# A block stack on one core: order of pieces of 16 and 32 passes, shifted copies issued from ScalarE's queue, feed-forward norms on ScalarE

## The chip, the core and the metric

The kernel runs on one core of a Trainium2 chip. The core's engines work side by side, each through its own instructions in order, and wait for each other through semaphores: TensorE (PE, with its weight loads PEld), VectorE (DVE), ScalarE (ACT), GpSimd (POOL) and SyncE (SP), which here issues most DMA transfers. The metric is the device time of one execution in microseconds; the time before is the median of three runs.

## The reference

Sixteen sequences of 256 tokens, 128 wide, in float32, pass through four residual blocks: softmax attention, a mixture of experts, retention, and a stack of six layers. The change touches the stack alone. One layer of it, cut:

```python
def attn_layer(x, Wqkv, qs, ksc, Wo):
    q, k, v = split(x @ Wqkv)                  # 16 heads of 64
    q = l2norm(q) * qs; k = l2norm(k) * ksc
    q = q * cos * scale + rotate_half(q) * sin * scale
    k = k * cos * inv + rotate_half(k) * sin * inv
    # windows of 32 queries see their own 32 keys and the 32 before
    attn = softmax(where(mask, -max, 8 * q @ k.T))
    return (attn @ v) @ Wo

def ffn_layer(x, g, bln, W1, b1, W2, b2):
    xn = (x - mean) / sqrt(var + 1e-5) * g + bln
    a, gate = split(xn @ W1 + b1)              # 2 x 341
    return a * gelu(gate) @ W2 + b2

for i in range(6):
    x = attn_layer(shift_tokens(x), ...) + x
    x = ffn_layer(shift_tokens(x), ...) + x
```

`shift_tokens` moves half of the channels by one token.

## The kernel before, in words

The first three blocks run until about 778 us. Then the stack begins. A unit (`Unit`) is the attention of one sequence in one layer: 6 layers x 16 sequences = 96 units. A `Forward` is the feed-forward part of two sequences. Their work is cut into named steps (methods), and the order of all steps is written out by hand as the words of `ORDER`: `pqk.1.0:4` means method `pqk` with arguments 1 and 0 for unit 2j + 4, in turn j of the loop (j from -3 to 50). One turn thus handles two sequences, each word at its own depth in the pipeline, and the engines' queues follow this order. The steps:

- TensorE: `pqk` (L916) makes queries or keys of four heads; `nr` (L950) sums the squares for the norms; `pv` (L994) makes values; `s_` (L1028) the scores, many small passes of 32 x 32; `pt` (L1083) transposes the probabilities; `o` (L1106) multiplies them with the values, in passes of 64 x 64; `y` (L1125) projects back. Of the feed-forward: `fn` (L1151) transposes, `trf` (L1185) transposes the normed values, `fg`, `fa` (L1204, L1217) and `fy` (L1234) are its three products. Each float32 matmul other than a transpose appears as two passes in the trace; `s_` and `o` as called before are 32 matmuls each, 64 passes, as is one `nr`.
- VectorE: `t2` and `rot` (L930, L935) for the rotation, `sm`, `mx`, `su`, `rec`, `nm` for the softmax, `rnA` and `rnC` for the norms, `xsu` (L1135) and `xsf` (L1249) add to the residual; `st` (L1163) takes the feed-forward's statistics and `z` (L1179) applies them.
- ScalarE: `sq` (L924) squares, `exp` (L1063), `rnB` (L965, a square root), `gl` (L1210, gelu), and copies out of PSUM: `vc` (L1003) values, `pTc` (L1091) probabilities, `oTc` (L1118) outputs, `nat` (L1157), `fz` (L1191).
- GpSimd: `add` (L941), `norm` (L988), `sub` (L1059), `rs` (L1169).
- SyncE's DMA queue: `bcD` (L975, L981) spreads a unit's norms over the partitions through DRAM, nine transfers; `vs` (L1010) copies parts of the values into a second place shifted by one window of 32 tokens, four transfers of 32 partitions per call, two calls a unit; and the weights of the next layer (`load_*`, issued by `follow` when the last user of the old ones has been emitted).

What couples them: `o` of the first half of a sequence's tokens reads what `vs.0` copied, of the second half also `vs.1`. PSUM is full: `pqk` has two buffers, scores one (so the scores of one half of the heads wait for `sm` of the other), `o` one, and everything else (`pt`, `pv`, `nr`, `y`, `fn`, `trf`, `fg`, `fa`, `fy`) takes turns in two buffers of `ps_m`: the third to come waits until the first has been read out. The readers of one `pqk` tile (`sq`, `t2`, `rot`) follow each other. Transfers signal on eight semaphores in rotation, and each issue waits until the transfer eight before it has landed.

Of the kernel before, what the change touches and what calls it, by code (L numbers as in the profile page):

```python
# [111 lines left out]
def kernel(ctx: ExitStack, tc: tile.TileContext, a: dict, widths: dict, out: bass.AP):  # L112
# [762 lines left out]
        nc.sync.dma_start(out=w, in_=a["wo2"][l].rearrange("p (c n) -> p c n", c=8))  # L875
        return w

    def load_ff(l):
        w1 = kc.tile([P, 2 * FF], F32, tag="w1", name=f"w1_{l}")
        w2 = kc.tile([P, 3, D], F32, tag="w2", name=f"w2_{l}")  # L880
        nc.sync.dma_start(out=w1, in_=a["w1"][l])
        nc.sync.dma_start(out=w2[:, 0:2, :], in_=a["w2"][l, 0:256].rearrange("(c p) n -> p c n", p=P))
        nc.sync.dma_start(out=w2[0 : FF - 256, 2, :], in_=a["w2"][l, 256:FF])
        return w1, w2

    class Unit:
# [55 lines left out]

        def nr(self, part):
            nr = self.misc("nr")[:, 0:64]
            for b in range(4 * part, 4 * part + 4):
                for hf in range(2):
                    for G in range(4):
                        nc.tensor.matmul(  # L950
                            nr[32 * G : 32 * G + 32, :],
                            lhsT=gather[:, b, :],
                            rhs=self.squares(G)[:, :, hf, WIN * b : WIN * b + WIN],
                            start=(b == 0 and hf == 0),
                            stop=(b == 7 and hf == 1),
                        )
# [48 lines left out]
        def vs(self, tt):  # L1005
            v = self.v_t
            for r in range(4):
                rows = slice(32 * r, 32 * r + 32)
                at, n = 2 * tt, 1 if tt and r % 2 else 2
                nc.sync.dma_start(out=v[rows, 1, at + r % 2 : at + r % 2 + n], in_=v[rows, 0, at : at + n])  # L1010

        def p_s(self, hu):
            return self.tile(ps_s, [P, 2, 2, 2, 2, 2 * WIN], "s", hu, tag="s")

        def s_(self, hu, tt, gh):
            ps, qk = self.p_s(hu), self.qk_t
            for G in (2 * gh, 2 * gh + 1):
                for hf in range(2):  # L1020
                    for b in range(4):
                        for r2 in range(2):
                            rows = slice(32 * (2 * hu + r2), 32 * (2 * hu + r2) + 32)
                            at = WIN * (4 * tt + b)
                            keys = qk[G][rows, 1, hf, at : at + 2 * WIN]
                            if b % 2 == 0:
                                keys = keys.rearrange("f (n t) -> f n t", n=2)[:, ::-1, :]
                            nc.tensor.matmul(  # L1028
                                ps[32 * b : 32 * b + 32, r2, tt, G // 2, G % 2, :],
                                lhsT=qk[G][rows, 0, hf, WIN + at : 2 * WIN + at],  # L1030
                                rhs=keys,
                                start=(hf == 0),
                                stop=(hf == 1),
                            )


        def t_sm(self, hu):
# [56 lines left out]
        def p_o(self, tt):  # L1094
            return self.tile(ps_o, [P, 2, 4, P], "o", tt, tag="o")

        def o(self, hu, tt):
            o, pT = self.p_o(tt), self.t_pT(hu, tt)
            for m in range(2):
                for b in range(4):  # L1100
                    for e in range(2):
                        for p in range(2):
                            rows = slice(64 * p, 64 * p + 64)
                            j = 2 * m + e
                            at = j * P + WIN * b
                            nc.tensor.matmul(  # L1106
                                o[64 * e : 64 * e + 64, p, 2 * hu + m, WIN * b : WIN * b + WIN],
                                lhsT=self.v_t[rows, 1 - b % 2, 2 * tt + b // 2, 4 * hu + j, :],
                                rhs=pT[rows, at : at + WIN],
                                start=True,  # L1110
                                stop=True,
                            )

        def t_oT(self):
            return self.tile(s2, [P, 8, T], "oT", bufs=1)
# [21 lines left out]
    class Forward(Unit):  # L1137
# [29 lines left out]
        def rs(self):  # L1167
            rs = self.tile(s2, [P, 4], "rs")
            nc.gpsimd.tensor_tensor(rs, rs, mhalf[:, 0:4], ALU.pow)  # L1169
            if self.last:  # L1170
                nc.sync.dma_start(out=self.tile(s2, [P, 4, D], "f_res", bufs=2), in_=kept[self.g])

# [1 line left out]
            return self.tile(s2, [P, 4, D], "ln_z")  # L1174

        def z(self):
            nat, mv, rs = self.t_nat(), self.tile(s2, [P, 4, 2], "ln_mv"), self.tile(s2, [P, 4], "rs")
            for k in range(4):
                nc.vector.tensor_scalar(  # L1179
                    self.t_z()[:, k, :], nat[:, k, :], mv[:, k, 0:1], rs[:, k : k + 1], ALU.subtract, ALU.mult  # L1180
                )

        def trf(self):
# [16 lines left out]

        def fg(self, n):
            f0, m = FFC[n]
            w1 = weights["ff", self.l][0]
            nc.tensor.matmul(  # L1204
                self.misc("fg", n)[0:m, :], lhsT=w1[:, FF + f0 : FF + f0 + m], rhs=self.t_zT(), start=True, stop=True
            )
# [6 lines left out]

        def fa(self, n):
            f0, m = FFC[n]
            w1 = weights["ff", self.l][0]
            nc.tensor.matmul(  # L1217
                self.misc("fa", n)[0:m, :], lhsT=w1[:, f0 : f0 + m], rhs=self.t_zT(), start=True, stop=True
            )
# [12 lines left out]
        def fy(self):  # L1232
            for n, (_, m) in enumerate(FFC):
                nc.tensor.matmul(  # L1234
                    self.misc("fy"),
                    lhsT=weights["ff", self.l][1][0:m, n, :],
                    rhs=self.t_h()[0:m, n, :],
                    start=(n == 0),
                    stop=(n == 2),
                )  # L1240
# [23 lines left out]


    ORDER = """
        add.1:3 o.0.0:0 sq.1.0:3 pqk.3.1:3 vs.1:0 fn:-2 rot.0.1:3 norm.1:2 pTc.1.1:0 t2.0.1:3 rot.3.1:3 sm.1:1
        sq.0.1:3 nat:-2 o.1.0:0 norm.0:2 rec.0:1 pqk.3.0:3 t2.3.0:3 oTc.0.1:0 pv.2:1 oTc.0.0:0 t2.3.1:3 o.0.1:0
        rot.3.0:3 pv.0:1 sq.3.1:3 s.0.0.0:2 add.0:3 sq.3.0:3 nm.0:1 mx.1:1 st:-2 vc.2:1 pqk.2.1:3 pv.3:1 sq.2.1:3
        o.1.1:0 pqk.2.0:3 vc.3:1 norm.3:2 sq.2.0:3 sub.1:1 norm.2:2 s.0.1.0:2 vc.0:1 t2.2.1:3 rot.2.1:3 pqk.1.0:4  # L1270
        pv.1:1 exp.1:1 nr.0:3 t2.2.0:3 nr.1:3 rs:-2 vc.1:1 su.1:1 rot.2.0:3 rec.1:1 rnA:3 rnB:3 pt.0.0:1 rnC:3 z:-2
        pqk.1.1:4 s.0.0.1:2 trf:-2 pTc.0.0:1 pt.0.1:1 s.0.1.1:2 fz:-2 pTc.0.1:1 nm.1:1 fy:-4 sm.0:2 oTc.1.0:0 bcD:3
        s.1.0.0:2 add.3:3 fg.0:-2 gl.0:-2 xsf:-4 t2.1.0:4 sq.1.1:4 s.1.1.0:2 t2.1.1:4 rot.1.0:4 mx.0:2 pt.1.1:1 pv.0:2
        pTc.1.1:1 vs.0:1 oTc.1.1:0 add.2:3 vc.0:2 s.1.0.1:2 rot.1.1:4 pt.1.0:1 y.0:0 sq.1.0:4 s.1.1.1:2 sub.0:2
        pqk.0.1:4 exp.0:2 norm.0:3 norm.1:3 pqk.0.0:4 sm.1:2 rot.0.1:4 o.0.0:1 sq.0.1:4 t2.0.1:4 add.1:4 su.0:2 y.1:0
        rec.0:2 xsu:0 pTc.1.0:1 mx.1:2 o.1.0:1 pv.3:2 t2.0.0:4 oTc.0.1:1 sub.1:2 pqk.3.1:4 nm.0:2 s.0.0.0:3 fa.0:-2
        oTc.0.0:1 rot.0.0:4 fh.0:-2 vc.3:2 sq.3.1:4 fg.1:-2 sq.0.0:4 exp.1:2 vs.1:1 o.0.1:1 fa.1:-2 o.1.1:1 rot.3.1:4
        pqk.3.0:4 gl.1:-2 t2.3.1:4 su.1:2 sq.3.0:4 norm.2:3 pqk.2.1:4 oTc.1.1:1 s.0.1.0:3 norm.3:3 rec.1:2 add.0:4
        fh.1:-2 pt.0.0:2 pTc.0.0:2 fg.2:-2 oTc.1.0:1 t2.3.0:4 s.0.1.1:3 pt.0.1:2 t2.2.1:4 rot.3.0:4 rot.2.1:4
        pqk.2.0:4 s.0.0.1:3 gl.2:-2 nm.1:2 pTc.0.1:2 sq.2.1:4 sq.2.0:4 sm.0:3 t2.2.0:4 rot.2.0:4 pv.1:2 vc.1:2 nr.0:4  # L1280
        mx.0:3 add.3:4 pqk.1.1:5 nr.1:4 rnA:4 pqk.0.0:5 s.1.1.0:3 t2.1.1:5 rnB:4 fa.2:-2 rnC:4 pv.2:2 bcD:4 sq.0.0:5
        sub.0:3 fh.2:-2 s.1.0.0:3 y.0:1 rot.1.1:5 sq.1.1:5 pqk.1.0:5 add.2:4 s.1.0.1:3 rot.0.0:5 t2.0.0:5 y.1:1
        exp.0:3 t2.1.0:5 vs.0:2 rot.1.0:5 vc.2:2 s.1.1.1:3 su.0:3 pt.1.0:2 pqk.0.1:5 xsu:1 pt.1.1:2 pTc.1.0:2
    """.split()

    weights = {}
# [10 lines left out]
    def follow(unit, method, args):  # L1297
# [11 lines left out]
        elif method == "t2" and q == 7 and count[key] == 1:  # L1309
            weights["rot", l + 1] = load_rot(l + 1)  # L1310
        elif method == "pv" and q == 9 and count[key] == 1:
            weights["v", l + 1] = load_v(l + 1)
        elif method == "y" and q == NSEQ - 1 and count[key] == 2:
            weights["o", l + 1] = load_o(l + 1)
        elif method == "fy" and q == NSEQ - 2:
            weights["ff", l + 1] = load_ff(l + 1)

    with tc.manual_schedule():
        for G in range(4):
# [1 line left out]
        weights["rot", 0] = load_rot(0)  # L1321
        weights["v", 0] = load_v(0)
        weights["o", 0] = load_o(0)
        weights["ff", 0] = load_ff(0)
        for j in range(-3, len(units) // 2 + 3):
            for method, args, d in steps:
                u = 2 * j + d
# [70 lines left out]
```

## Time and profile before

| | before |
|---|---|
| median of three runs | 4451.55 us (4458.10, 4432.63, 4451.55) |
| profiled execution, its own time | 4439.28 us |
| start of the first and of the last `pqk` | 778.1 and 4320.1 us |
| granted TensorE clock over the whole execution | 0.948 |
| ScalarE's table loads of `exp`, `rnB`, `gl` | 96, 95 and 93, 1.28 us each |
| DVE L1179 z, 192 of 128x128 | 90.0 us busy |
| DMA v<-v on SyncE's queue | 768 transfers, issue 507 ns at least, 582 in the middle |
| SyncE waiting for `rnC` (L968) ahead of `bcD` | 2084 us in all |

The share of an engine says how long it was busy, not that it set the end. In a list of waits a line reads: who waited, for whom, the microseconds in total, how often, and the longest. In a timeline each line has the start, the time, the engine, the line of code, the operation and the tiles, and in brackets the engine's idle time just before and what ended it; `x64` says that 64 instructions were merged. In a table of windows the columns are the stretch, its length, the busy time of PE, PEld, DVE, ACT and POOL (with counts), the granted TensorE clock as a share of full speed, the busy share of the DMA engines, and GB/s.

### The profile page before, as it was taken

The page shows a single profiled execution, that of the slowest core. Times are in us where ns is not written, and L with a number is a line of the kernel's source. Part 1 is how long each engine was busy: PE and PEld are TensorE (multiplying, and loading weights), DVE is VectorE, ACT ScalarE, POOL GpSimd, SP SyncE. Part 2 cuts the span into 40 slices and gives each one's busy share as a digit, 9 for nine tenths or more (in the row PEclk, how much of TensorE's full clock was granted, in tenths as well). Part 3 has the DMA queues.
Part 4 walks back from the last instruction along what each step waited for, and adds up shares of the span by engine and source line. Part 5 has one row for each costly group of instructions (what it writes and reads, how often), then busy time and mean ns, then how long its engine had stood idle before and what let it go on. Part 6 is the DMA issues. An engine that isn't in the chain of part 4 may idle for free.

```text
span 4437.5 us, 216472 instructions
## 1 busy us (share of the span) xinstructions
PE 4129.3 (93%) x100320; PEld 2826.1 (64%) x100320; DVE 2976.0 (67%) x5436; ACT 2078.2 (47%) x3342; POOL 2528.5 (57%) x1419
## 2 busy tenths in 40 slices
PE   5888886799999999999999999999999999999998
PEld 3555664466666666666666666666666666666665
DVE  4555553567777667776777676777677777667774
ACT  2334432244545445544455454455454555444543
POOL 2433333556666656665666666666666666666661
PEclk9879777789999999999999999999999999999999
DMA  3200000222222222222222222232322232222222
GB/s 114 79 27 22 14 6 9 69 67 58 63 63 62 66 69 62 58 67 62 64 66 61 69 55 56 65 74 49 75 51 74 55 75 58 64 59 65 65 65 51
DMA packets 208901, 260.85 MB, mean 59 GB/s; under 512 B 54143, under 2 KB 164605, under 8 KB 207101
## 3 DMA queue, kind: packets, MB, share of 16 engines
q1 hardware_dynamic: 204796, 243.38, 21.8%
q8 instruction: 787, 12.89, 1.3%
q10 hardware_dynamic: 3200, 3.62, 0.3%
q14 instruction: 118, 0.96, 0.1%
HBM read 140.98 MB, written 17.83 MB: 36 GB/s over the span
## 4 chain that ended last, share of the span: by engine, by line
PE 69%; DVE 10%; DMA 7%; POOL 5%; issue 3%; SPq 3%; ACT 3%; ACTq 0%; POOLq 0%; DVEq 0%
PE pqk L916 13%; PE s L1028 10%; PE o L1106 8%; PE pv L994 7%; PE y L1125 6%; DMA v<-v 4%; PE nr L950 4%; PE pt L1083 3%; PE fy L1234 3%; PE fa L1217 2%; PE fg L1204 2%; POOL qk L988 2%; PE st L271 2%; DVE sm L1077 2%; SPq L981 2%
## 5 line engine op out<-in xcount | busy, mean ns | idle before, releaser
L941 POOL TENSOR_TENSOR qk<-qk,t 128x1024 f32<-128x1024 f32 x384 | 907.1, 2366 | 303.7 <-DVE qk L935 299.6
L988 POOL TENSOR_TENSOR qk<-qk,bc 128x1024 f32<-128x1024 f32 x384 | 948.6, 2488 | 95.3 <-DMA v<-v 77.9
L1059 POOL TENSOR_TENSOR sm<-sm,mx 128x1024 f32<-128x1024 f32 x192 | 366.2, 1907 | 954.1 <-PE pt L1083 331.2
L916 PE MATMUL pqk<-xs,wqk 128*128 128x256 f32 x3072 | 847.7, 405 | 30.3 <-ACT sq L924 14.6
L1028 PEld LDWEIGHTS s<-qk 32*32 32x32 f32 x49152 | 537.1, 104 | 394.8 <-issue 371.4
L924 ACT ACTIVATE sq<-pqk 128x512 f32<-128x512 f32 x768 | 454.5, 599 | 688.0 <-DVE qk L935 364.9
L930 DVE TENSOR_TENSOR t<-pqk,rot 128x512 f32<-128x512 f32 x768 | 521.0, 685 | 279.3 <-ACT sq L924 135.5
L935 DVE TENSOR_TENSOR qk<-pqk,rot 128x512 f32<-128x512 f32 x768 | 514.6, 681 | 279.6 <-PE pqk L916 224.6
L1028 PE MATMUL s<-qk 32*32 32x64 f32 x49152 | 664.9, 223 | 16.8 <-POOL qk L988 7.5
L916 PEld LDWEIGHTS pqk<-xs,wqk 128*128 128x128 f32 x3072 | 546.4, 194 | 156.4 <-issue 56.0
L1106 PEld LDWEIGHTS o<-pT,v 64*64 64x64 f32 x24576 | 420.5, 139 | 289.6 <-issue 159.3
L1106 PE MATMUL o<-pT,v 64*64 64x32 f32 x24576 | 470.8, 224 | 77.3 <-DMA v<-v 76.0
L1091 ACT COPY pT<-pt 128x512 f32<-128x512 f32 x384 | 224.6, 585 | 446.2 <-PE pt L1083 235.9
L994 PE MATMUL pv<-wv,xs 128*64 128x512 f32 x1536 | 420.2, 626 | 0.0
L1077 DVE TENSOR_TENSOR sm<-sm,rec 128x1024 f32<-128x1024 f32 x192 | 418.7, 2181 | 0.0
L1125 PE MATMUL y<-oT,wo 128*128 128x256 f32 x1536 | 384.8, 394 | 0.3 <-ACT pT L1091 0.3
L1044 DVE TENSOR_TENSOR sm<-s,c_ident 128x1024 f32<-128x1024 f32 x192 | 233.9, 1218 | 143.0 <-PE s L1028 142.0
L1125 PEld LDWEIGHTS y<-oT,wo 128*128 128x128 f32 x1536 | 280.8, 193 | 43.9 <-ACT f_gl L1210 0.8
L1118 ACT COPY oT<-o 128x512 f32<-128x512 f32 x384 | 216.2, 589 | 160.7 <-PE o L1106 160.7
L1003 ACT COPY v<-pv 128x512 f32<-128x512 f32 x384 | 224.6, 585 | 131.2 <-PE pv L994 131.2
L286 POOL TENSOR_SCALAR_AFFINE_SELECT pe<-pe 128x512 f32<-128x512 f32 x128 | 81.7, 640 | 331.9 <-ACT pe L279 316.1
L1067 DVE TENSOR_REDUCE su<-sm 128x16 f32<-128x1024 f32 x192 | 232.4, 1210 | 38.7 <-ACT sm L1063 38.7
(188 smaller groups left out, 5298.5 us busy)
## 6 DMA issues: line engine op xcount, KB each, us to landing
bc<-ndr SPq DMA_DIRECT2D x768, 128.0 KB
v<-v SPq DMA_DIRECT2D x576, 128.0 KB
v<-v SPq DMA_DIRECT2D x192, 64.0 KB
rot_l<-in_rot_dram SPq DMA_DIRECT2D x12, 512.0 KB
rot<-rot_l SPq DMA_DIRECT2D x12, 512.0 KB
wqk<-in_wqk_dram SPq DMA_DIRECT2D x24, 256.0 KB
rot<-rot SPq DMA_DIRECT2D x6, 1024.0 KB
wv<-in_wv_dram SPq DMA_DIRECT2D x6, 512.0 KB
```

What stands on the lines that cost most here:

```text
L916: nc.tensor.matmul(self.p_qk(G, k)[:, hf, :], lhsT=weights["qk", G, self.l][:, k, hf, :], rhs=xq, start=True, stop=True)
L924: nc.scalar.activation(self.squares(G)[:, k], self.p_qk(G, k), AF.Square)
L930: nc.vector.tensor_tensor(self.t_2(G)[:, k], self.p_qk(G, k)[:, ::-1, :], weights["rot", self.l][:, 1, k], ALU.mult)
L935: nc.vector.tensor_tensor(self.qk_t[G][:, k, :, WIN : WIN + T], self.p_qk(G, k), weights["rot", self.l][:, 0, k], ALU.mult)
L941: nc.gpsimd.tensor_tensor(to, to, self.t_2(G), ALU.add)
L988: nc.gpsimd.tensor_tensor(to, to, self.bcast()[:, G, :, None, :].to_broadcast([P, 2, 2, T]), ALU.mult)
L994: nc.tensor.matmul(self.misc("pv", i)[64 * p : 64 * p + 64, :], lhsT=xs[self.g][:, self.s, cols], rhs=weights["v", self.l][:, p, :], start ...
L1028: nc.tensor.matmul(ps[32 * b : 32 * b + 32, r2, tt, G // 2, G % 2, :], lhsT=qk[G][rows, 0, hf, WIN + at : 2 * WIN + at], rhs=keys, start=( ...
L1059: nc.gpsimd.tensor_tensor(s3, s3, self.t_mx(hu)[:, :, None].to_broadcast([P, 16, 2 * WIN]), ALU.subtract)
L1077: nc.vector.tensor_tensor(s3, s3, self.t_rec(hu)[:, :, None].to_broadcast([P, 16, 2 * WIN]), ALU.mult)
L1106: nc.tensor.matmul(o[64 * e : 64 * e + 64, p, 2 * hu + m, WIN * b : WIN * b + WIN], lhsT=self.v_t[rows, 1 - b % 2, 2 * tt + b // 2, 4 * hu ...
L1125: nc.tensor.matmul(self.misc("y")[:, 0:T], lhsT=weights["o", self.l][:, ch, :], rhs=self.t_oT()[:, ch, :], start=(ch == 0), stop=(ch == 7),)
```

## The change

It does five things, all in the stack:

1. `s_`, `o` and `nr` are called for half as much each: `s_` for one group of heads (16 matmuls), `o` for one part (16), `nr` for two windows (16). Their matmuls are the same.
2. `vs` issues its four copies from ScalarE's queue.
3. `z` is four ScalarE activations with a scale and a bias in place of four VectorE operations; `rs` computes the bias with two more small GpSimd instructions.
4. `load_ff` is parted into `load_w1`, emitted after the layer's last `fg` or `fa`, and `load_w2`, emitted after `fy` as before.
5. `ORDER` is new: 243 words for 215. The depths still run from -4 to 5.

```diff
-            for b in range(4 * part, 4 * part + 4):
+            for b in (2 * part, 2 * part + 1):
...
-                nc.sync.dma_start(out=v[rows, 1, at + r % 2 : at + r % 2 + n], in_=v[rows, 0, at : at + n])
+                nc.scalar.dma_start(out=v[rows, 1, at + r % 2 : at + r % 2 + n], in_=v[rows, 0, at : at + n])
...
-        def s_(self, hu, tt, gh):
-            ps, qk = self.p_s(hu), self.qk_t
-            for G in (2 * gh, 2 * gh + 1):
-                for hf in range(2):
+        def s_(self, hu, tt, G):
+            ps, qk = self.p_s(hu), self.qk_t[G]
+            for hf in range(2):
...
-        def o(self, hu, tt):
+        def o(self, hu, tt, part):
             o, pT = self.p_o(tt), self.t_pT(hu, tt)
-            for m in range(2):
-                for b in range(4):
+            for b in range(4):
...
             nc.gpsimd.tensor_tensor(rs, rs, mhalf[:, 0:4], ALU.pow)
+            nb, mv = self.tile(s2, [P, 4], "nb"), self.tile(s2, [P, 4, 2], "ln_mv")
+            nc.gpsimd.tensor_tensor(nb, mv[:, :, 0], rs, ALU.mult)
+            nc.gpsimd.tensor_scalar(nb, nb, -1.0, None, ALU.mult)
...
             for k in range(4):
-                nc.vector.tensor_scalar(
-                    self.t_z()[:, k, :], nat[:, k, :], mv[:, k, 0:1], rs[:, k : k + 1], ALU.subtract, ALU.mult
+                nc.scalar.activation(
+                    self.t_z()[:, k, :], nat[:, k, :], AF.Identity, bias=nb[:, k : k + 1], scale=rs[:, k : k + 1]
                 )
...
-    def load_ff(l):
+    def load_w1(l):
...
+        elif method in ("fg", "fa") and q == NSEQ - 2:
+            both = (l, "w1")
+            count[both] = count.get(both, 0) + 1
+            if count[both] == 6:
+                weights["w1", l + 1] = load_w1(l + 1)
         elif method == "fy" and q == NSEQ - 2:
-            weights["ff", l + 1] = load_ff(l + 1)
+            weights["w2", l + 1] = load_w2(l + 1)
```

The new `ORDER`, its first and its last words (the seam between two turns) and the place of the even sequence's copies:

```
t2.3.1:3 rot.3.1:3 o.0.1.1:0 pqk.2.1:3 trf:-2 s.0.1.2:2 s.0.1.1:2 rot.2.1:3 sub.1:1 sq.2.1:3 vs.0:1 fz:-2
vs.1:1 pt.0.0:1 add.1:3 pqk.2.0:3 t2.2.1:3 s.0.0.1:2 s.0.1.0:2 add.3:3 pt.0.1:1 oTc.1.0:0 pqk.1.0:4 sq.2.0:3
pTc.0.0:1 nr.0:3 s.0.0.3:2 rot.2.0:3 pTc.0.1:1 sm.0:2 oTc.1.1:0 nr.1:3 mx.0:2 exp.1:1 y.0:0 nr.2:3 nr.3:3
...
oTc.1.1:1 mx.0:3 s.1.1.0:3 vs.0:2 s.1.0.1:3 y.1:1 sq.0.0:5 s.1.0.0:3 s.1.1.1:3 pqk.0.1:5 pt.1.0:2 s.1.0.2:3
xsu:1 s.1.1.3:3 pTc.1.0:2 rot.0.0:5 sub.0:3 vs.1:2 fa.2:-2 add.2:4 fn:0 t2.0.1:5 t2.0.0:5 o.0.0.1:2 rot.0.1:5
...
norm.2:4 s.0.0.2:4 rs:0 norm.3:4 pqk.3.1:5 nm.0:3 norm.0:4 pv.1:3 s.0.0.0:4 s.0.1.3:4 sq.3.1:5 pv.2:3
o.1.1.1:2 norm.1:4 vc.1:3 rot.3.0:5 vc.2:3 t2.3.0:5 z:0
```

and in the old one the even sequence's first copies and the first `o` that reads them, over the seam:

```
exp.0:3 t2.1.0:5 vs.0:2 rot.1.0:5 vc.2:2 s.1.1.1:3 su.0:3 pt.1.0:2 pqk.0.1:5 xsu:1 pt.1.1:2 pTc.1.0:2
add.1:3 o.0.0:0 ...
```

## The prediction

> **What bounds the kernel now.** I read the page first, then who waited for whom on TensorE in the steady part of the stack (1000 to 4250 us), then the timeline around the longest of those waits, then the granted clock in short stretches. The page:
>
> ```profile
> span 4437.5 us, 216472 instructions
> PE 4129.3 (93%) x100320; PEld 2826.1 (64%) x100320; DVE 2976.0 (67%) x5436; ACT 2078.2 (47%) x3342; POOL 2528.5 (57%) x1419
> PE 69%; DVE 10%; DMA 7%; POOL 5%; issue 3%; SPq 3%; ACT 3%; ACTq 0%; POOLq 0%; DVEq 0%
> ```
>
> TensorE is the bound; no other engine passes 67%. The change's time is therefore read as TensorE's: its pieces back to back, plus its waits. One turn of the loop (two sequences) is the distance from one fn to the next. The 44 fn of that stretch begin at 1031.7 and end at 4233.1 us, so a turn is (4233.1 - 0.3 - 1031.7)/43 = 74.4 us, and 48 turns are 3571 us. TensorE's own waits there, and the stretch's clock:
>
> ```profile
> PE o L1106 <- DMA v<-v: 68.7, 66, 4.2
> PE trf L1185 <- DVE ln_z L1179: 11.3, 25, 0.6
> ```
> ```profile
> 1000.00:4250.00 3250.00, 3156.61 (x86406) 2159.23 (x86404) 2355.45 (x3414) 1632.15 (x2490) 2049.57 (x919) 0.99 0.26 63
> 2515.60:2522.30 6.70, 6.44 (x134) 5.58 (x134) 1.98 (x3) 1.67 (x3) 6.70 (x4) 0.50 0.19 45
> 2819.20:2822.60 3.40, 2.65 (x70) 2.23 (x71) 0.00 (x0) 0.91 (x2) 3.40 (x2) 1.00 0.30 75
> 2822.60:2826.00 3.40, 3.40 (x77) 2.14 (x75) 2.67 (x5) 1.84 (x4) 3.40 (x3) 1.00 0.02 5
> ```
>
> The only large wait is that of o for the shifted copies of the values. Their timeline, SyncE above TensorE:
>
> ```profile
> 2511.06 0.51 SPq L1010 DMA_DIRECT2D v<-v  x1
> 2512.42 0.36 SPq L859 DMA_DIRECT2D wqk<-in_wqk_dram  x1
> 2513.83 2.41 SPq L1010 DMA_DIRECT2D v<-v  x4
> ...
> 2515.24 0.30 PE L1106 MATMUL o<-pT,v 64*64 64x32 f32 x2 [2.42 <-DMA v<-v]
> 2515.86 1.92 PE L1106 MATMUL o<-pT,v 64*64 64x32 f32 x62 [0.33 <-DMA v<-v]
> ```
>
> The copies stand in SyncE's queue among weights, and after 2.42 us of idling TensorE ran 6.7 us at half clock (0.50 above). The copies' 1.28 and 0.66 us of idling at 2818 to 2820 us left the clock at 1.00 (the two rows after). So a stall over some 1.7 us is paid twice.
>
> **Part 1, copies off SyncE.** In the new order vs.0:2 is followed by ten pieces before the first o that reads it (a y half, a pqk, a pt, fa, fn and five s halves: 1.83 + 0.96 + 0.5 + 1.05 + 0.53 + 5 x 0.39, about 7 us of TensorE against s, pt, pqk, pt, 2.7 us, before), and the copies pass weights and the norm's transfers in SyncE's queue. I take the wait as gone: 68.7/43.6 turns = 1.6 us a turn, and with it the half clock. The clock of 0.99 over 3250 us is 16 to 49 us lost (rounding); I take 44, as single stalls lose 3 us each: 1.0 us a turn. Gain 2.6, bounds 0 and 2.7.
>
> The Trainium skill speaks against this (DMA: Bandwidth & Descriptors, "Issuing engines are not separate DMA queues"): transfers started by any engine run on the same 16 DMA engines and interleave, and only the sequencer's time is saved. If that alone were so the copies would still land late and this gain would be nothing; the timeline above shows the issue itself late, behind other issues, which the move does cure.
>
> **Part 2, smaller pieces.** Every s, o and nr is cut in two: 28 more pieces a turn (16, 8 and 4). From start to start in a quiet stretch:
>
> ```profile
> 2446.49 1.14 PE L1106 MATMUL o<-pT,v 64*64 64x32 f32 x64
> 2447.55 1.08 PE L994 MATMUL pv<-wv,xs 128*64 128x512 f32 x4
> 2448.56 0.85 PE L1028 MATMUL s<-qk 32*32 32x64 f32 x64
> 2449.35 1.13 PE L916 MATMUL pqk<-xs,wqk 128*128 128x256 f32 x4
> 2450.41 1.08 PE L994 MATMUL pv<-wv,xs 128*64 128x512 f32 x4
> ```
>
> An o takes 1.06, an s 0.79, a pv 1.01, a pqk 1.06 us. Between the last start in a piece of s or o and the next piece's lies about 0.15 us. That handover is what a cut adds. In the new order 16 of the 28 new ends are followed by a piece of the same kind (10 s, 4 o, 2 nr), which hands over nothing, so 12 remain: at most 12 x 0.15 = 1.8 us a turn; at least nothing, as the rest of TensorE's work is the same pieces. I take 0.7: o and nr (six ends, 0.9) nearly full, s nearly nothing, as by the single starts in the trace the first 32 passes of an s go out in 0.27 us and the last 32 in 0.37, so that two first halves are cheaper than one whole.
>
> **Part 3, norms on ScalarE.** z leaves VectorE (192 x 0.335 to 0.53 us) for four activations of the kind of z_s, 1.65 us a turn; GpSimd gets two instructions of 4 columns, 0.20 and 0.24 us (rows of nb). VectorE and GpSimd have idle time, so neither counts by itself; GpSimd's 0.45 stands ahead of three norms whose s come about 0.6 us after them by the rows; without that cover it costs 0.45. trf waited 0.26 us a turn for z before and, with z behind vc.2, waits about as long. The order also parts gl and exp: eight table loads a turn instead of six, 2 x 1.28 us on ScalarE, under other pieces.
>
> **Part 4, what stands behind the copies on ScalarE.** 16 issues a turn move there. ScalarE's prices:
>
> ```profile
> 771.77 1.65 ACT L173 ACTIVATE z_s<-xn,nb_s,rs_s 128x128 f32<-128x128 f32 x4 [7.23 <-POOL nb_s L165]
> ...
> 774.36 0.35 ACTq L835 DMA_DIRECT2D vecs<-in_vecs_dram  x1
> 774.36 0.37 ACT L619 COPY xs<-tr_s 64x256 f32<-64x256 f32 x1
> ```
>
> One issue beside queued copies held nothing up. Four of v<-v took SyncE 2.41 us, and 16 make 9.6 us on an engine busy some 37 of 74 us: room enough over a turn. The place that hurts is the turn's seam, where vs.0 and vs.1 of the odd sequence stand on both sides of fz, ahead of sq.2.0 and pTc.0.0. nr needs both (the second because it frees nr's PSUM slot), and all later work waits behind nr. Counted from the end of pv.2. ScalarE: vc 0.59, z 1.65 = 2.24; sq.2.1 must wait for rot.2.1, 2.85; four copies 2.41 = 5.3; fz beside the next four, 7.7; oT, sq, pT 0.6 each, overlapping slightly = 9.4. TensorE: two o halves 1.07, pqk 0.96, trf 0.5, two s halves 0.79, pt 0.5, pqk 0.96, s 0.79, pt 0.5, pqk 1.06 = 7.1. nr is 2.3 us late each turn (part of it already at pt.0.1, which needs fz). Bounds: 0.7 if an issue takes 0.35 as the one above; 3.5 if the issues overlap neither sq nor fz. I take 2.3, since SyncE's row is of the same transfer. Elsewhere (vs.0:2 and vs.1:2 in mid-turn) the same count leaves ScalarE ahead of TensorE.
>
> **Part 5, the clock after that stall.** Some 1.7 us of it fall in one piece at nr, just where the clock broke above. A fall is 3.4 us at half, 1.7 us; I take one in four turns: 0.4, bounds 0 and 1.7. The Trainium skill's TensorE: Matmul & The Clock Gate ("Why this matters for your kernels") asks only that idle gaps stay under about 3 us; by it this term would be nothing. The 2.42 us gap above already halved the clock, so I keep the row.
>
> w1 is now fetched after the last fa, w2 after fy, and SyncE waits less long at both; fill and drain keep their depth (-4 to 5). I count nothing for these, with 15 us either way.
>
> **Sum.** -2.6 + 0.7 + 2.3 + 0.4 = +0.8 us a turn, x 48 = +38 us. The profiled execution took 4439.3 (span 4437.5): 4478. The median of the three runs is 4451.55, 1.0028 times that execution: 4490 us.
>
> **Rivals.** (a) Faster: ScalarE's sequencer runs ahead, issues cost 0.35, and nr is 0.7 us late with no fall of the clock: -2.6 + 0.7 + 0.7 = -1.2, x 48 = -58, 4393 on the median's scale. It decides once nr's wait is under 1.4 us. For it: the issue that hid above. Against: four in a row find at most one queued operation to hide behind. (b) No change: nr is 1.9 late and the clock holds, 0 a turn: 4452. (c) Worse: the clock falls at every seam, -2.6 + 0.7 + 2.3 + 1.7 = +2.1, 4553. (d) The move does not do what it says: copies still land late, so the 2.6 stays: +3.4, 4615; against it, 7 us of cover.
>
> **How the numbers follow.** Forecast 0.30, (a) 0.30, (b) 0.22, (c) 0.13, (d) 0.05. A measurement of this kernel tells about 0.5% (22 us) from no change: faster 0.30, same 0.22, slower 0.48. Range 4375 to 4580: it takes in (a) to (c) and leaves (d) and an (a) without any stall outside; the forecast's own is 4470 to 4560.
>
> **What would show it.** v<-v gone from TensorE's waits (part 1); o's halves at 0.53 to 0.6 us from start to start (part 2); ScalarE's fz and sq.2.0 behind rows of ACTq v<-v of 2.4 us, and nr waiting for ACT once a turn (part 4); half-clock stretches after nr, or none (part 5). It is wrong if nr's wait is under 1.4 us, or if other pieces begin to wait for ScalarE.

## The result, and the profile after

The changed kernel takes 4701.88 us in the median (four runs, 4679.18 to 4705.94), the kernel before beside it 4454.83: a ratio of 1.0547, with a 95% interval of 1.0488 to 1.0606. Slower was forecast as the likeliest direction, but by 38 us; it is 247, far outside the range.

The page of the changed kernel (span; engines' busy time; the chain of work that ended last):

```profile
span 4704.2 us, 216628 instructions
...
PE 4216.4 (90%) x100320; PEld 2864.7 (61%) x100320; DVE 2775.0 (59%) x5244; ACT 2280.3 (48%) x3626; POOL 2584.2 (55%) x1515
...
PE 75%; DVE 6%; ACTq 4%; DMA 4%; POOL 4%; ACT 4%; issue 2%; SPq 1%; POOLq 0%; DVEq 0%
```

TensorE's share fell from 93 to 90% with the same 100,320 passes in a longer span, so new waits came in. Who TensorE waited for from 1000 to 4500 us (us in total, times, longest):

```profile
PE s L1030 <- POOL qk L991: 110.4, 29, 8.4
PE nr L953 <- ACT pT L1093: 87.9, 43, 3.3
PE pt L1085 <- ACT f_zT L1195: 47.0, 38, 2.2
```

`o` for `v<-v`, the one large wait of before, is gone from this list, as predicted. The second and third lines are the predicted seam: once a turn, behind ScalarE. The first line nobody had asked about: the scores wait for GpSimd's `norm` in 29 places, up to 8.4 us. And the clock (stretch, length, busy times, granted clock, DMA share, GB/s) fell:

```profile
1000.00:4100.00 3100.00, 2871.35 (x76785) 1950.13 (x76784) 1918.79 (x2872) 1619.12 (x2447) 1867.96 (x895) 0.95 0.24 59
1361.00:1382.00 21.00, 17.55 (x324) 11.13 (x324) 2.71 (x5) 5.84 (x12) 15.57 (x10) 0.60 0.27 68
```

The same 3100 us had 0.99 before. The time lost at half clock, added up over all records at 0.50 from 1000 to 4250 us (half of each one's length), is 150 us for 44. The second row shows where it goes: 21 us behind one 8.4 us wait.

Where is that wait? The length of a turn tells, from its first piece on TensorE to that of the next turn. Turns with j = 8l + 5, 8l + 7 and 8l + 8 are those in which a layer's last `pqk`, `y` and `fa` are issued, after each of which weights of the next layer are loaded (l from 0 to 4; means worked out from the starts in the traces):

| mean turn, us | regular | 8l+5 (`wqk`) | 8l+7 (`wo`) | 8l+8 (`w1`) | 8l+9 (`w2`; before `w1` too) |
|---|---|---|---|---|---|
| before | 73.0 | 74.9 | 75.1 | 74.9 | 79.2 |
| changed | 76.4 | 88.7 | 82.0 | 87.8 | 77.0 |

The last class is that of a layer's last `fy`, after which the old kernel loaded `w1` and `w2`; "regular" are the turns 8l + 2, 3, 4 and 6 up to 42. The regular turns grew by 3.4 us. The first three classes of a layer's boundary exceed them by 12.3 + 5.6 + 11.4 = 29 us, five times 147, where before they exceeded theirs by 6. The fourth fell: it exceeded the regular turns by 6.2 us before and by 0.6 now. With it the boundaries cost 12.1 us a layer before and 29.9 now, 89 us more in five layers; the 3.4 us of 48 turns are 163, and the two make about the 247 measured. One boundary in the timeline (start, time, engine, line, operation, and in brackets the idle time before and what ended it):

```profile
1340.54 5.94 SPq L859 DMA_DIRECT2D wqk<-in_wqk_dram  x2
...
1346.57 0.39 SPq L978 DMA_DIRECT2D ndr<-rn  x1
...
1350.47 4.78 SPq L984 DMA_DIRECT2D bc<-ndr  x8
...
1359.39 2.34 POOL L991 TENSOR_TENSOR qk<-qk,bc 128x1024 f32<-128x1024 f32 x1 [13.81 <-DMA bc<-ndr]
...
1361.78 0.68 PE L1030 MATMUL s<-qk 32*32 32x64 f32 x32 [8.41 <-POOL qk L991]
```

SyncE issues the two `wqk` loads first, then `ndr`, then `bc`; GpSimd has been idle 13.8 us for `bc`, TensorE 8.4 us for GpSimd. The norms that `ndr` reads had been ready since 1332.6, 14 us before its issue. SyncE's own waits from 1000 to 4100 us, changed kernel:

```profile
SPq L859 <- PE pqk L919: 305.4, 20, 34.6
SPq L875 <- PE y L1126: 157.0, 5, 32.7
SPq L880 <- PE fa L1221: 135.2, 4, 34.3
```

and before:

```profile
SPq L882 <- PE fy L1234: 121.9, 5, 24.9
SPq L859 <- PE pqk L916: 72.7, 13, 7.6
...
SPq L875 <- PE y L1125: 8.6, 5, 2.7
```

SyncE stands up to 34 us ahead of a load whose buffer TensorE still reads. The old order did this above all at one load, `w2`'s: in the turn j = 9 SyncE stands ahead of it from 1547.5 to 1571.5, then issues `ndr`, `bc` and eight copies, and `o` waits up to 3.5 us for the copies. That is the 79.2 us class. In the new order the same kind of wait is at three loads, and ahead of the scores: the word `bcD:4`, which spreads the even sequence's norms, comes after `pqk.0`, `pqk.1`, `y.1` and `fa.2`, though `rnC:4` was done long before. When no weights are due, SyncE reaches `bcD` early and its place costs nothing; at a boundary it costs the whole wait.

The seam, in the timeline of a regular turn:

```profile
2412.18 0.60 ACT L927 ACTIVATE sq<-pqk 128x512 f32<-128x512 f32 x1 [0.71 <-DVE qk L938]
2412.24 3.57 ACTq L1013 DMA_DIRECT2D v<-v  x4
...
2415.86 0.78 ACT L1195 ACTIVATE f_zT<-trf,vecs 128x512 f32<-128x512 f32 x1 [3.08 <-DMA v<-v]
2415.93 2.44 ACTq L1013 DMA_DIRECT2D v<-v  x4
...
2416.69 0.66 PE L1085 MATMUL pt<-c_ident,sm 128*128 128x128 f32 x4 [1.82 <-ACT f_zT L1195]
...
2419.39 1.08 ACT L1093 COPY pT<-pt 128x512 f32<-128x512 f32 x2
...
2420.03 0.65 PE L953 MATMUL nr<-sq,c_ident 128*32 128x64 f32 x32 [1.82 <-ACT pT L1093]
```

The chain is the predicted one, link by link; only the first four copies take 3.57 us in this turn instead of 2.41 (2.44 to 3.9 over the turns, 3.0 in the mean), and `pt` already waits.

### The profile page after: what moved, and what is told of

It is laid out like the page before. It is cut to its first block, busy times and chain, and to the rows that moved or that the text cites. A ratio compares the mean times of both kernels' runs of the same rounds, so it can differ in the third digit from the quotient of the medians.

```text
span 4704.2 us, 216628 instructions
## 1 busy us (share of the span) xinstructions
PE 4216.4 (90%) x100320; PEld 2864.7 (61%) x100320; DVE 2775.0 (59%) x5244; ACT 2280.3 (48%) x3626; POOL 2584.2 (55%) x1515
## 4 chain that ended last, share of the span: by engine, by line
PE 75%; DVE 6%; ACTq 4%; DMA 4%; POOL 4%; ACT 4%; issue 2%; SPq 1%; POOLq 0%; DVEq 0%
PE pqk L919 14%; PE s L1030 11%; PE o L1107 8%; PE y L1126 8%; PE pv L997 7%; PE nr L953 5%; ACTq L1013 4%; PE fg L1208 3%; PE pt L1085 3%; PE fa L1221 3%; PE fy L1238 3%; POOL qk L991 2%; PE st L271 2%; DMA v<-v 2%; DVE qk L938 1%
## 5 line engine op out<-in xcount | busy, mean ns | idle before, releaser
L991 POOL TENSOR_TENSOR qk<-qk,bc 128x1024 f32<-128x1024 f32 x384 | 978.4, 2573 | 171.3 <-DMA bc<-ndr 164.7
L919 PE MATMUL pqk<-xs,wqk 128*128 128x256 f32 x3072 | 882.8, 414 | 24.5 <-issue 7.0
L1030 PE MATMUL s<-qk 32*32 32x64 f32 x49152 | 689.9, 226 | 132.4 <-POOL qk L991 122.2
L1030 PEld LDWEIGHTS s<-qk 32*32 32x32 f32 x49152 | 512.6, 106 | 423.6 <-issue 251.7
L1107 PE MATMUL o<-pT,v 64*64 64x32 f32 x24576 | 490.4, 224 | 2.5 <-issue 2.0
L1126 PE MATMUL y<-oT,wo 128*128 128x256 f32 x1536 | 413.3, 416 | 2.2 <-ACT pT L1093 2.2
L1126 PEld LDWEIGHTS y<-oT,wo 128*128 128x128 f32 x1536 | 297.5, 204 | 59.2 <-issue 2.7
L953 PE MATMUL nr<-sq,c_ident 128*32 128x64 f32 x12288 | 236.3, 229 | 99.2 <-ACT pT L1093 98.9
L953 PEld LDWEIGHTS nr<-sq,c_ident 128*32 128x32 f32 x12288 | 194.7, 115 | 197.4 <-ACT pT L1093 120.0
L1085 PE MATMUL pt<-c_ident,sm 128*128 128x128 f32 x1536 | 250.2, 287 | 54.1 <-ACT f_zT L1195 51.4
```

The lines of the kernel that those rows point to most:

```text
L919: nc.tensor.matmul(self.p_qk(G, k)[:, hf, :], lhsT=weights["qk", G, self.l][:, k, hf, :], rhs=xq, start=True, stop=True)
L953: nc.tensor.matmul(nr[32 * G : 32 * G + 32, :], lhsT=gather[:, b, :], rhs=self.squares(G)[:, :, hf, WIN * b : WIN * b + WIN], start=(b == ...
L991: nc.gpsimd.tensor_tensor(to, to, self.bcast()[:, G, :, None, :].to_broadcast([P, 2, 2, T]), ALU.mult)
L1030: nc.tensor.matmul(ps[32 * b : 32 * b + 32, r2, tt, G // 2, G % 2, :], lhsT=qk[rows, 0, hf, WIN + at : 2 * WIN + at], rhs=keys, start=(hf ...
L1085: nc.tensor.transpose(pt[:, j * P : (j + 1) * P], sm[:, j // 2, tt, j % 2].rearrange("n p c -> n (p c)"), ident)
L1107: nc.tensor.matmul(o[64 * e : 64 * e + 64, p, 2 * hu + part, WIN * b : WIN * b + WIN], lhsT=self.v_t[rows, 1 - b % 2, 2 * tt + b // 2, 4 * ...
```

## The experiments

Three theories for the extra time: Q, SyncE's queue at the boundaries; S, ScalarE at the seam with the clock after it; H, handovers of the 28 additional pieces. In the diffs of `ORDER` each word has a line of its own. The stretch of all lists of waits is 1000 to 4100 us, that of the half-clock loss 1000 to 4250.

**bcD moved forward (Q alone).**

```diff
 rnC:4
+bcD:4
 s.0.0.3:3
...
 su.0:3
-bcD:4
 sq.1.1:5
```

> Changed kernel with one word moved: bcD of the even sequence (ndr and bc on SyncE's queue) directly after rnC, ahead of the weights that follow pqk, y and fa. Theory Q (SyncE's queue): at the five layer boundaries weights that wait for TensorE hold ndr and bc back, the norms on GpSimd come late and s waits (turns of 82 to 90 us for 76, some 31 us a boundary). Then this takes 100 to 155 us off: 4545 to 4600 us, and the waits of s for qk (110 us from 1000 to 4500) fall under 30. Theory S (ScalarE's seam: nr and pt behind the copies, and the clock after them, are the whole loss): at most 30 us off, 4670 to 4700, and the long turns stay. Theory H (the 28 more pieces hand over dearly): no change in the turns' lengths, 4690 to 4715.

4546.16 us (4529.75 to 4553.25), 1.0214 of before (1.0173 to 1.0255): 156 us off. The boundary turns are 75.2, 76.1 and 77.2 us beside 76.2 for the others. TensorE's two longest entries are now

```profile
PE nr L953 <- ACT pT L1093: 84.7, 40, 3.4
PE pt L1085 <- ACT f_zT L1195: 47.1, 40, 2.2
```

and `s` for `qk` is not among them. Half-clock loss is 51 us instead of 150: two thirds of it came from the boundaries. The time is in the range of theory Q, at its lower end; S and H alone are out. Another wait of SyncE at `ndr` is not the cause: it waits for `v<-v` through the shared semaphores 764 us in the changed kernel (36 times) and 760 here (40 times), and here `s` does not wait.

**The odd sequence's copies moved out of the seam (S alone).**

```diff
 sq.2.1:3
-vs.0:1
 fz:-2
-vs.1:1
 pt.0.0:1
...
 pTc.0.1:1
+vs.0:1
 sm.0:2
...
 sq.1.1:4
+vs.1:1
 pv.0:2
```

> Changed kernel with the odd sequence's two words vs moved out of the seam, to after pTc.0.1 and after sq.1.1, where ScalarE has room. Theory S: the waits of nr for pT (88 us from 1000 to 4500) and of pt for f_zT (47 us) go, and half of the half-clock time (150 us lost) with them: 135 + 60, so 4490 to 4540 us. Theory Q: only the regular turns shorten, by 2.9 us of wait at most and no clock (46 turns: 130 us at most), and the long turns at the boundaries stay: 4570 to 4640. Theory H: 4690 to 4715. If instead o begins to wait for v<-v, the move has only shifted the stall.

4532.02 us (4530.07 to 4533.49), 1.0187 (1.0153 to 1.0221): 170 us off. The waits for `pT` and `f_zT` are gone; what stays is

```profile
PE s L1030 <- POOL qk L991: 108.1, 32, 7.9
PE pt L1085 <- ACT f_gl L1214: 28.0, 40, 1.8
```

The time is in the range of theory S and below that of Q. Regular turns fell from 76.4 to 72.6 us; boundary turns, at 84.2, 79.5 and 84.0, stay as much longer than these. So both theories hold, each for its own turns. The second line is new: moved to ahead of `gl.0`, four issues make `pt.1.0` 0.6 us late each turn.

**Both moves.**

> Both moves together. If Q and S are two separate losses they add up: the two gains of the other runs within 40 us, 4370 to 4440 us, which would be faster than the kernel before. If one hides behind the other (the same stall seen twice), the sum falls short by over 60 us.

4368.22 us (4362.34 to 4383.89), 0.9825 of before (0.9787 to 0.9863). Alone the moves took 156 and 170 us, together 334: they add up (2 us below the range expected for that), and the kernel is now faster than before. The clock over the stretch, and `s` for `qk`:

```profile
1000.00:4100.00 3100.00, 3049.94 (x84438) 2077.27 (x84419) 2142.59 (x3157) 1780.09 (x2689) 2057.98 (x983) 1.00 0.26 65
```
```profile
PE s L1030 <- POOL qk L991: 1.0, 2, 0.6
```

TensorE got through 84,438 passes in the stretch in which the changed kernel did 76,785 and before 82,325.

**The changed kernel with the copies back on SyncE.** Line 1013 as `nc.sync.dma_start`.

> Changed kernel with the copies back on SyncE's queue, all else as changed. Theory S: nr's and pt's waits for ScalarE go (135 us and their clock, some 60), but the copies pass weights and bc again: where the o that reads them has 7 us of cover they are hidden in regular turns; 4510 to 4560 us. Theory Q: SyncE's queue, with 16 issues a turn more (9.3 us), is later still at the boundaries: 4650 to 4750, and o waits for v<-v at the boundaries.

4734.98 us (4730.67 to 4748.97), 1.0650 (1.0604 to 1.0697): 33 us slower than changed. The seam's waits go, but

```profile
PE s L1030 <- POOL qk L991: 221.5, 68, 8.0
```
```profile
SPq L1013 <- ACT v L1006: 1416.5, 77, 28.8
```

SyncE now stands ahead of the copies until ScalarE has made their values, and `bcD` behind them is late in nearly every turn: regular turns 79.2 us. The time is in the range of theory Q, but `o`, which by that theory would wait for `v<-v`, does not; theory S, with 4510 to 4560, missed the time.

**Both moves, copies on SyncE.**

> The run with both moves, but with the copies on SyncE's queue: is the move to ScalarE worth anything by itself? Theory I (the issue's place counts: on SyncE sixteen issues of some 0.6 us stand ahead of ndr and bc, or wait for vc and hold them, as in the run with the copies on SyncE alone, where s waited 221 us for the norms): s waits for qk in most turns, 2 to 5 us a turn with its clock, 4470 to 4600 us. Theory N (the engine that issues doesn't matter, transfers share the same DMA engines): 4355 to 4385, as with the copies on ScalarE.

4420.69 us (4419.69 to 4436.1), 0.9946 (0.9926 to 0.9965): 52 us more than with ScalarE, and neither expectation hit. `s` does not wait, as `bcD` is now ahead of the copies; instead

```profile
PE o L1107 <- DMA v<-v: 50.8, 84, 1.9
```

0.6 us in 84 places. Half-clock loss is 40 us, for 3 with ScalarE and 44 before. The issuing engine is thus worth 52 us here; without it the new order with its other edits is 27 us (0.5%) faster than before.

**Both moves, z back on VectorE (part 3 undone).** Lines 1171 to 1173 out, `z` as before.

> The run with both moves, but z on VectorE again and without the two small GpSimd instructions (part 3 undone). The prediction counted part 3 as nothing: 4355 to 4385 us. If ScalarE is short of time after the move (pt waits 0.6 us a turn for f_gl), it gains up to that: 4335 to 4355. If VectorE is the tighter engine, 4385 to 4420.

4505.16 us (4503.84 to 4527.73), 1.0138 (1.0107 to 1.0168): 137 us slower, a miss for all three. The group of `z` (count, busy us, mean ns), TensorE's wait for it, and one `z` in the timeline beside GpSimd:

```profile
L1180 DVE TENSOR_SCALAR ln_z<-f_nat,ln_mv,rs 128x128 f32<-128x128 f32 x192 | 251.7, 1370 | 1.1 <-POOL rs L1170 1.1
```
```profile
PE trf L1186 <- DVE ln_z L1180: 59.6, 38, 2.0
```
```profile
2394.76 3.37 POOL L991 TENSOR_TENSOR qk<-qk,bc 128x1024 f32<-128x1024 f32 x1
...
2397.01 5.61 DVE L1180 TENSOR_SCALAR ln_z<-f_nat,ln_mv,rs 128x128 f32<-128x128 f32 x4
...
2398.09 1.90 POOL L1061 TENSOR_TENSOR sm<-sm,mx 128x1024 f32<-128x1024 f32 x1
...
2399.95 2.34 POOL L944 TENSOR_TENSOR qk<-qk,t 128x1024 f32<-128x1024 f32 x1
```

A `z` takes 0.335 us in the mean where GpSimd does nothing (58 of the 192) and 1.82 where it works (134); each of the 134 ends 0.08 to 0.09 us after an instruction of GpSimd. In its new place GpSimd is busy through nearly all of it, so the four above take 5.61 us, in the rhythm of GpSimd's instructions: the ends of these, 2398.1, 2400.0 and 2402.3, are when the next `z` gets through, and the fourth ends at 2402.6. Half-clock loss goes to 60 us from 3.

**The kernel before with the copies on ScalarE's queue (part 1 alone).** Line 1010 of before as `nc.scalar.dma_start`.

> The kernel before with one line changed: the copies issued from ScalarE's queue (part 1 alone, in the old order, which has 2.7 us of TensorE between the copies and the first o instead of 7). Prediction's part 1 (the wait is the late issue behind other issues on SyncE; 1.6 us of wait and 1.0 of clock a turn go): 4330 to 4370 us, and o waits for v<-v under 15 us from 1000 to 4250. If the order's cover is what cured it, o still waits, 4430 to 4460. If ScalarE stalls behind the issues in this order too: over 4470, and pt, nr or s wait for ACT.

4870.02 us (4863.16 to 4887.97), 1.0958 (1.0923 to 1.0993): 422 us slower.

```profile
PE o L1106 <- DMA v<-v: 145.8, 94, 3.4
PE y L1125 <- ACT v L1003: 64.9, 37, 2.8
PE pqk L916 <- DVE qk L935: 31.8, 33, 1.8
```

In the old order two of the four calls of `vs` in a turn stand just behind an `exp` and two closely ahead of a `vc`, and `o` follows soon. `o` waits more than twice as long as on SyncE (67.3 before in this stretch), `y` waits for `vc`, and the half-clock loss is 184 us. The time is in the third range expected, though the pieces that wait are `o` and `y` and not `pt`, `nr` or `s`. The move alone cures nothing.

**Both moves, vs.1 after gl.0.**

```diff
 sq.1.1:4
-vs.1:1
 pv.0:2
...
 gl.0:-2
+vs.1:1
 bcD:3
```

> The run with both moves, but the second call of the odd sequence's copies after gl.0 instead of ahead of it, so that pt.1.0 no longer waits for f_gl behind four issues (28.8 us from 1000 to 4100, 0.62 a turn). If that wait is all they cost: 30 us less, 4335 to 4350. If they then hold pT or exp back: pt or o waits for ACT pT, 4360 to 4400.

4339.41 us (4328.87 to 4346.15), 0.9751 (0.9727 to 0.9774), as expected from the 0.62 us a turn: 29 us less, and the fastest version of all. `pt` for `f_gl` has left the list; regular turns are 71.6 us.

**Half of the seam's copies put back: vs.0, or vs.1.** To this fastest version, first `vs.0:1` back between `sq.2.1:3` and `fz:-2`, then, in another run, `vs.1:1` back behind `fz:-2`.

> The fastest run so far (both moves, vs.1 of the odd sequence after gl.0; 4339 us), with vs.0 of the odd sequence back at the seam ahead of fz, as in the changed kernel: half of the copies that stood there. By the prediction's count ScalarE is at 5.3 after these four copies, 5.9 after fz and 7.6 after oT, sq and pT, for TensorE's 7.1: nr is 0.5 late each turn and the clock holds, 24 us: 4355 to 4380, half-clock time under 30 us. If the seam's loss goes by the number of copies (170 us for eight): 4410 to 4440. If one late fz alone makes the loss: 4470 to 4520, and pt waits for f_zT as in the changed kernel.

> The same, but vs.1 of the odd sequence at the seam behind fz, as in the changed kernel, and vs.0 out of it. By the prediction's count fz is done at 3.5, the copies at 5.9, oT, sq and pT at 7.6, for 7.1: nr 0.5 late, pt not late, 4355 to 4380. If the loss goes by the number of copies: 4410 to 4440. If fz makes the loss: 4330 to 4350.

With vs.0: 4412.06 us (4382.26 to 4417.58), 0.9907 (0.9874 to 0.9939), 73 us more than without (52 between the profiled executions, over the 42 turns from 4 to 45), two to three times the count. With vs.1: 4354.85 (4348.96 to 4373.95), 0.9805 (0.9769 to 0.9841), 15 us more, near the count. The first falls into the range for a loss by the number of copies, but the second, with as many copies, does not: what counts is which piece stands behind them. TensorE's first entry in each:

```profile
PE pt L1085 <- ACT f_zT L1195: 46.5, 42, 1.9
```
```profile
PE nr L953 <- ACT pT L1093: 19.9, 21, 1.5
```

The count's walk, laid on a turn of the trace with vs.0 at the seam, shows what was short:

```profile
2441.23 1.65 ACT L1183 ACTIVATE ln_z<-f_nat,nb,rs 128x128 f32<-128x128 f32 x4
2443.59 0.60 ACT L927 ACTIVATE sq<-pqk 128x512 f32<-128x512 f32 x1 [0.71 <-DVE qk L938]
2443.65 3.05 ACTq L1013 DMA_DIRECT2D v<-v  x4
2446.76 0.78 ACT L1195 ACTIVATE f_zT<-trf,vecs 128x512 f32<-128x512 f32 x1 [2.56 <-DMA v<-v]
```

`vc` started at 2440.75, and `sq.2.1` starts 2.84 us later (counted 2.85). The issues take 3.05 us here and 2.87 in the mean of 42 turns, 2.44 to 3.67 (counted 2.41), and `fz` 0.78 (counted some 0.6): in the mean 0.46 + 0.18 = 0.6 us more than counted, which on top of a counted 0.4 at `pt.0.1` makes about the 46.5 / 42 = 1.1 us measured. Half-clock loss is 19 us with vs.0 and 10 with vs.1, for 15 without either: stalls of 1.1 and 0.5 us a turn in the mean hardly touched the clock.

**The changed kernel, only w1's load behind bcD; then all loads behind it.** `bcD` stays in its late place; the loads that stood ahead of it are emitted just after it.

```diff
             if count[both] == 6:
-                weights["w1", l + 1] = load_w1(l + 1)
+                later.append((l, None))
...
+        while method == "bcD" and q % 2 == 0 and later:
+            k, G = later.pop(0)
+            weights["w1", k + 1] = load_w1(k + 1)
```

The second run does the same with `wo` and groups 0 and 1 of `wqk`.

> The changed kernel with the load of w1 alone emitted after bcD of the even sequence instead of ahead of it; bcD stays where it is. Theory Q (each load that waits for TensorE ahead of bcD makes its own turn longer): only the turns in which w1 is loaded, 8k+8, shorten, from 87 to 76 us, five times: 4702 - 55 = 4630 to 4660. If the three loads share one cause (or the traffic of the weights does it): 4685 to 4715.

> The changed kernel with bcD where it is and all loads ahead of it (two of wqk, wo, w1) emitted after it. Theory Q (the wait in SyncE's queue, not bcD's own place in the order and not the weights' traffic): the same as moving bcD forward, 4546 us, within 20; s waits for qk under 30 us from 1000 to 4100. If bcD's own late place or the traffic counts: 4600 or more.

w1 alone: 4634.38 us (4627.9 to 4660.32), 1.0438 (1.0396 to 1.0479), 67 us off. Its turns 8l+8 are 77.3 us for 87.8, the other two classes 87.5 and 81.8 as in the changed kernel. All loads: 4541.38 us (4533.98 to 4558.07), 1.0221 (1.0179 to 1.0264), which is what moving `bcD` gave; turns of 75.2, 76.1 and 77.3 us, and `s` for `qk` gone:

```profile
PE nr L953 <- ACT pT L1093: 84.7, 41, 3.5
PE pt L1085 <- ACT f_zT L1195: 49.6, 41, 2.2
```
```profile
SPq L859 <- PE pqk L919: 79.8, 15, 8.1
```

The same loads move the same bytes and cost nothing here. Each load ahead of `bcD` makes its own turn longer, and neither `bcD`'s own place nor the weights' traffic does.

## Why the prediction was wrong, step by step

**The step that failed: the weights.** The prediction said that "w1 is now fetched after the last fa, w2 after fy, and SyncE waits less long at both", and counted nothing, 15 us either way. For `w2` that held: SyncE's wait ahead of it fell from 121.9 us to 18.4, and its turn from 79.2 us to 77.0. For the others it did not: the waits for `pqk`, `y` and `fa` grew from 81 us together to 598. The prediction compared each load with its own last reader and never asked what stands behind the loads in SyncE's queue. The answer is `bcD`, and behind it the norms and `s`. That is worth 156 us (bcD forward) or 160 (loads behind it), three quarters of the 212 us between 4490 and 4702. SyncE's waits at the loads had been in the trace of before; the new order was there to be laid beside them.

**Part 4, the seam: right in place, too small.** Links, waiting pieces and releaser are as written. With `bcD` moved, `nr` and `pt` wait 131.8 us over 3100 us, which is 41 turns: 3.2 us a turn for 2.3 predicted and 3.5 as the upper bound. The mis-sized terms are the issues, priced at 2.41 us for four, and `fz`. It is not that ScalarE issues more slowly: from 1000 to 4250 us four copies take 2.44 to 4.17 us on its queue (mean 2.90, changed kernel) and 2.41 to 4.11 on SyncE's (mean 2.99, before). The row that the prediction took is among the shortest of 174.

**Part 5, the clock: too small, by the same cause and by the weights.** Predicted 0.4 us a turn with a bound of 1.7. With the boundaries cured the half-clock loss is 51 us over 42.6 turns, 1.2 a turn; without the seam's copies too it is 3 to 15 us over the whole stretch. The rule quoted there from the Trainium skill (TensorE: Matmul & The Clock Gate, "Why this matters for your kernels"), gaps under some 3 us, would have left this term at nothing; stalls of which the longest is 3.4 us cost some 40, and only 7 of the 24 half-clock stretches there have a wait of 3.0 us or more just ahead, so the row of before was the better guide. But "a stall over some 1.7 us is paid twice" is not a rule either: of single waits of 1.7 to 2.0 us half clock followed within 3.5 us on 4 of 4 before, and on 2 of 26 with `bcD` moved (the last section has more). The larger share, 150 - 51 = 99 us, followed the boundary stalls. Not all of it need be added time, as slower pieces may fill what would otherwise be waits; no run separates the two. Parts 4 and 5 together came to 170 to 178 us (copies out of the seam, alone and after `bcD`) for (2.3 + 0.4) x 48 = 130, and to 207 against the fastest version, where the moved copies hold nothing up.

**Part 1: the wait gone, the reason half right.** The wait of `o` is gone, as predicted. But with the copies on ScalarE in the old order it doubled (145.8 us), and with the copies on SyncE in the new order, `bcD` and the seam mended, it is 50.8 us for 67.3 before, with 40 us of half-clock loss for 44. Neither the cover nor the queue cures it alone; together they do, and the queue's share is then 52 us. The rule of the Trainium skill that was weighed there (DMA: Bandwidth & Descriptors, "Issuing engines are not separate DMA queues") is not contradicted: what changed is when the issue takes place.

**Part 2: the lower end.** By pairs of neighbouring pieces, each at its 10th percentile, TensorE's work without waits is 69.7 us a turn in the changed kernel and 69.9 before, where a pair is named by its two methods. With every pair of words kept apart and the idle time taken off, it is 71.0 and 70.6. So the additional ends cost between nothing and half a microsecond; 0.7 was predicted, between 0 and 1.8. Theory H falls with it.

**Part 3: right only as it stands.** Nothing was counted for `z` on ScalarE, and no run contradicts that for the change as a whole. But with `z` on VectorE the new order costs 137 us more, as GpSimd works at that place. "VectorE and GpSimd have idle time, so neither counts" was the wrong reason: what counts is whether GpSimd runs at that moment.

**The sum.** Without parts 4 and 5 the prediction's terms are -2.6 + 0.7 = -1.9 us a turn, 48 x -1.9 = -91, about 4360 us. The run with both causes removed, but with the new 0.6 us wait at `pt`, measured 4368, and without that wait 4339. So outside the seam and the boundaries the terms together were good to some 0.4 us a turn, and the miss lies in 15 of 48 turns that it did not look at (156 us) and in the seam (some 45 us more than counted by the run with 4368, 77 by that with 4339). The rivals were all about the regular turn too. That loads and `bcD` form one queue was in none of them.

## What to carry to other kernels

When an order is rewritten, walk every in-order queue, DMA issue queues too, through the rare turns as well as the common one: list what stands behind each instruction that can wait, and who needs it. A word whose place costs nothing while the queue ahead is empty can cost a whole wait when a load is due. And price an issue by the spread of its rows and not by one of them, because one microsecond at a seam that all later work passes is paid every turn.

## What was not expected of the hardware

A VectorE instruction of 0.334 us took 1.82 us in the mean and 2.38 at the 90th percentile beside GpSimd's work, and finished only when an instruction of GpSimd ended. The Trainium skill describes this (SBUF — State Buffer, "Who interferes with whom"): the two engines share a pair of ports, which one of them holds for its whole instruction while the other is blocked; it counts a `tensor_scalar` among the forms that can want that pair. The rows of `z` agree with it.

Four issues of 32-partition copies took 2.4 to 4.2 us, on ScalarE's queue as on SyncE's, and the activations behind them on ScalarE waited for nearly all of it (3.08 of 3.57 us in the seam above); an issue could begin beside the activation just ahead (0.06 us after its start), so only the first overlaps.

After a wait of 8.4 us TensorE ran at a granted clock of 0.60 over the next 21 us: the half clock stood from 1357.2 to 1377.6 us, 20.5 us, for 6.8 around the 2.42 us wait of before. Waits of 1.1 us in the mean once a turn left the half-clock loss near where it was (19 us for 15).

In all fourteen traces of this case the half-clock stretches begin, from 900 us on, on a grid of 3.413 us that runs through the execution (none is off by more than 3 ns), and nearly all last a whole number of its steps. Taking the steps at full clock from 1000 to 4250 us together, by TensorE's records: half clock came next after each of the 154 in which it was idle for over 60% of the step, after none of the 11,932 with under 25%, and after 185 of the 613 between. A stall near 2 us can thus be paid twice or not; that this depends on whether it falls into one step or across two is inferred from the grid, and no run varies it.
